# Recurrence output in SBUF, a fourth PSUM bank for short products and a new order table, in a fused cross-attention and RWKV kernel

## The chip, the cores and the metric

The kernel runs on one core of a Trainium2 chip. The metric is the device time of one execution in microseconds (us). The kernel before takes 2110.64 us, the median of three runs (2108.8 to 2110.85).

The engines are called as in the profile: PE does matrix products (PEld are its weight loads), DVE and POOL work element by element, ACT evaluates functions and copies, and SP issues the transfers (DMA). PE writes only to PSUM, a small memory of eight banks; each bank holds 512 fp32 numbers in each of 128 partitions. All other tiles lie in SBUF.

## The reference

Two layers run one after the other on x (32 sequences of 128 rows, 512 wide), all in fp32. The first is cross-attention to `ctx` with a residual and a layer norm. The second, which the change touches, is an RWKV layer; H is 32 heads of S = 16:

```python
xn = _ln(x, ln1_w, ln1_b); sx = _token_shift(xn, state[:, i1])
xxx = tanh((xn + sx * maa_x) @ maa_w1) ... @ maa_w2          # five mixes
x5 = xn[:, :, None] + sx[:, :, None] * (maa_stack + xxx)
w = exp(-exp(time_decay + tanh(x5[1] @ decay_w1) @ decay_w2))
r, k, v = x5[3] @ Wr.T, x5[0] @ Wk.T, x5[2] @ Wv.T;  g = silu(x5[4] @ Wg.T)
def step(s, rkvw):                       # over the 128 rows
    a = k_t[:, :, :, None] * v_t[:, :, None, :]
    out = einsum('bhk,bhkd->bhd', r_t, u * a + s)
    return (a + w_t[:, :, :, None] * s, out)
# group norm over each head, * g, @ Wo.T, residual; then ln2, token shift,
# rr = sigmoid(xr @ Wr2.T); kk = square(relu(xk @ Wk2.T)); x + rr * (kk @ Wv2.T)
```

## The kernel before, in words

The 32 sequences go in 16 groups of two (`G` = 2, so 256 columns, `N`). The first layer runs through all groups; then the second layer does. For each group of the second layer there are three parts, written as functions that only record steps: `front` (norm, token shift, the five mixes `x5`, then the products for k, v, r, the gate and the decay), `recurrence`, and `tail` (group norm, output product, second norm, the three products of the channel mix, store).

**The recurrence** works in four chunks `c` of 128 channels. For each chunk ACT writes the decay into `w4` in PSUM (L1313, two banks, one buffer). Four times per chunk (`dd` = 0 to 3), SP has fetched v, repeated over partitions, into `kv` (L1356, three buffers, each for two `dd`). POOL multiplies it by k (L1379). DVE runs the recurrence over rows as one scan of 1024 columns, out of `w4` and `kv` into `a` (L1395). `a` takes two banks of PSUM and has one buffer. DVE multiplies `a` by r, read out of SBUF and repeated four times, into `ar` in SBUF (L1410, three buffers). After each two `dd`, PE sums `ar` over partitions into `acc` (L1426, one bank). Then DVE adds the current row's own term (L1444), PE centres it (`pc`, L1453), and ACT leaves two results (L1461, L1468).

**PSUM banks**: three for the tag `g`, which every short product of both layers shares (`px5`, `pk`, `pv`, `pr`, `pg`, `pd`, `pc`, `pb`, `ph0`, `pdd`, `pwo`, `pkk`, `prr`, `pkv`, the transposes `pxn`, and so on); two for `a`; one for `acc`; two for `w4`. The tile framework puts in all waits between engines. It also keeps two engines from using one bank of a tile at the same time: the copy of r out of `pr` on ACT (L737) and the product of the same `pr` with k on DVE (L745) are ordered one behind the other.

**The order of the work** is written out when the program is built. Each step has an engine, a work (an estimate of its time in us, from `mm`, `dve`, `act` and `pool_`) and a due time. `Plan.give_out` takes the steps one by one: of the steps whose inputs are made and whose tags have a free place, it takes the one that can start first by its own reckoning, within `ahead` of the oldest due time. Then every engine runs its instructions strictly in this order. The due times come from a table, `WHEN0` for the first layer and `WHEN1` for the second, with one number for each kind of step. The reckoning adds `AFTER` us between engines, and `SWITCH` us where PE changes the shape of its array ("full", "cols", "rows", "turn"). Steps with the tag `g` may take its places in any order (`FREE`).

During the first layer, `beside` puts the loading of the second layer's weights between the steps: transfers on SP (L1170, L1180, L1188) and, for the two weights whose columns change places, a copy on POOL (L1191), through the small pool `wt`.

Of the kernel before, what the change touches and what calls it, by code (L numbers as in the profile page):

```python
# [19 lines left out]
G = 2  # L20
# [57 lines left out]
        att 0: 0.4337, att 1: 0.2346, att 2: 0.4481, att 3: 42.2036, ew 0: 11.1338, ew 1: -0.2147, ew 2: 26.1389,  # L78
        ew 3: -0.1243, gt 0: 26.2110, gt 2: 2.1890, h0: 0.5241, hd: 0.3002, kk 0: 0.9228, kk 2: 20.4292,
        kv 0 0 0: 25.5890, kv 0 0 1: 21.9376, kv 0 1 0: 6.0558, kv 0 1 1: 0.8322, kv 1 0 0: 6.3560, kv 1 0 1: 29.3594,  # L80
        kv 1 1 0: 9.2616, kv 1 1 1: 25.6198, kv 2 0 0: 43.5542, kv 2 0 1: 7.4919, kv 2 1 0: 8.5948, kv 2 1 1: 43.5152,
        kv 3 0 0: 9.4194, kv 3 0 1: 22.4588, kv 3 1 0: 30.1517, kv 3 1 1: 12.4171, pk 0: 26.3643, pk 2: 24.3430,
        pv 0: 22.5942, pv 2: -0.1385, r 0: 26.3795, r 2: 23.3115, rr 0: 40.0790, rr 1: 27.6728, rstd: 26.0489,
        sq 0: -0.1128, sq 1: 23.3775, sq 2: 36.1033, sq 3: 41.1479, w4 0: 25.5550, w4 1: 21.3052, w4 2: 2.5964,
        w4 3: 27.6773, xnc 0: 8.8046, xnc 1: 1.2163, xnc 2: 4.5961, xnc 3: 10.3705, xnt 0: 37.5160, xnt 1: 36.3160,
        xnt 2: -1.1905, xnt 3: 3.6365, xx 0: 20.5242, xx 1: 34.9847, xx 2: 23.3521, xx 3: 22.4330, yk 0: 41.2808,
        yk 1: 20.7056, yk 2: 23.1054, yk 3: 23.1512, yr 0: 42.3101, yr 1: 3.1488, yr 2: 21.3085, yr 3: 2.7447,
        zc 0: 0.7541, zc 1: 27.0647, zt 0: 0.2936, zt 1: 22.7466
    """,
    "DVE": """  # L90
        a 0 0: 23.1285, a 0 1: 44.6967, a 0 2: 19.4777, a 0 3: 17.2122, a 1 0: 22.0121, a 1 1: 24.8715, a 1 2: 8.6631,
        a 1 3: 9.3222, a 2 0: 23.2268, a 2 1: 8.2943, a 2 2: 21.2763, a 2 3: 8.0300, a 3 0: 1.3330, a 3 1: 44.9810,
        a 3 2: 36.5134, a 3 3: 42.7805, ar 0 0: 1.0179, ar 0 1: 22.3833, ar 0 2: 27.7052, ar 0 3: 25.6817,
        ar 1 0: 37.2615, ar 1 1: 13.6436, ar 1 2: 22.7659, ar 1 3: 45.7511, ar 2 0: 6.0171, ar 2 1: 12.5578,
        ar 2 2: 28.8789, ar 2 3: 15.8516, ar 3 0: 23.3130, ar 3 1: 23.1491, ar 3 2: 19.9556, ar 3 3: 32.9812,
        gn 0: 23.7852, gn 1: 20.9580, gn 2: 33.5535, gn 3: 46.4228, gt 0: -0.0231, gt 2: -0.1977, own 0: 5.1099,
        own 1: 0.1224, own 2: -0.0283, own 3: 0.3349, pb 0: 8.0751, pb 1: 2.2968, pb 2: 0.8375, pb 3: 20.4024,
        raw 0: 23.2010, raw 1: 3.5965, raw 2: 23.2455, raw 3: 44.4584, rk 0: -0.7509, rk 1: -0.1719, rr 0: 1.6746,
        rr 1: 1.3382, rstd: 7.6463, st c 0: 11.1186, st c 1: 40.4898, st t 0: 28.5724, st t 1: 15.0321, x1c 0: 2.5303,
        x1c 1: 26.0962, x5 0 0: 2.7039, x5 0 1: 2.7955, x5 0 2: 24.3069, x5 0 3: 21.8074, x5 1 0: -0.0972,  # L100
        x5 1 1: 21.6197, x5 1 2: 0.6004, x5 1 3: 22.4358, x5 2 0: 42.1808, x5 2 1: -0.8591, x5 2 2: 41.2059,
        x5 2 3: 37.6158, x5 3 0: 26.8334, x5 3 1: 24.0914, x5 3 2: 23.6554, x5 3 3: 2.4313, x5 4 0: 25.8630,
        x5 4 1: 22.1314, x5 4 2: 40.0832, x5 4 3: 41.0197
    """,
    "PE": """
        acc 0: 22.3033, acc 1: 7.0581, acc 2: 22.7806, acc 3: 4.9952, pb 0: 27.7390, pb 2: 22.7260, pc 0: 2.0619,
        pc 1: 28.1521, pc 2: 3.1673, pc 3: 23.4917, pd 0: 33.6053, pd 1: 24.8921, pd 2: 20.8375, pd 3: 23.9500,
        pdd: -1.1093, pew 0: 23.8627, pew 2: 5.8633, pg 0: 23.5794, pg 2: 22.0824, ph0: -0.4813, pk 0: -1.0989,
        pk 2: -0.6925, pkk 0: 19.1077, pkk 2: 22.4386, pkv 0: 19.0064, pkv 1: 23.2658, pr 0: 1.2036, pr 2: 2.3445,
        prr 0: 1.8637, prr 1: 21.7968, pv 0: -0.8518, pv 2: 7.2890, pvar: 5.4151, pwo 0: 32.7897, pwo 1: 23.4460,  # L110
        px5 1 0: 39.8845, px5 1 2: 11.2421, px5 2 0: 23.4434, px5 2 2: 23.3758, px5 4 0: 0.9353, pxnc 0: 24.0019,
        pxnc 2: 21.6438, pxnt 0: -1.1522, pxnt 2: 13.7523
    """,
    "POOL": """
        kv 0 0 0: 26.0772, kv 0 0 1: 23.5502, kv 0 1 0: 27.7860, kv 0 1 1: 29.1526, kv 1 0 0: 0.4056,
        kv 1 0 1: 25.8430, kv 1 1 0: 5.7684, kv 1 1 1: 31.4921, kv 2 0 0: 28.2020, kv 2 0 1: 19.5485,
        kv 2 1 0: 29.7046, kv 2 1 1: 42.4003, kv 3 0 0: 10.6540, kv 3 0 1: 4.0853, kv 3 1 0: 25.5882,
        kv 3 1 1: 22.5557, rr 0: 2.4732, rr 1: 44.9550, sd c 0: 18.3198, sd c 1: 13.1243, sd t 0: 33.5214,
        sd t 1: 22.7124, sxc 0: 2.6017, sxc 2: 21.1060, sxt 0: 21.9776, sxt 2: -1.3154, x5 0 0: 41.1636,
        x5 0 2: 2.6161, x5 1 0: 34.2012, x5 1 2: 22.9652, x5 2 0: 22.8432, x5 2 2: 24.0895, x5 3 0: 23.6407,  # L120
        x5 3 2: 27.8090, x5 4 0: 41.2196, x5 4 2: 26.2718, xx 0: 24.1836, xx 2: 9.4476, yk 0: 24.7724, yk 2: 33.3339,
        yr 0: 1.5862, yr 2: 3.3642
    """,
    "SP": """
        fk: 43.5334, fr: 16.5653, kv 0 0 0: 26.7655, kv 0 1 0: 23.9392, kv 1 0 0: 24.5017, kv 1 1 0: 4.2079,
        kv 2 0 0: 5.4685, kv 2 1 0: 28.7358, kv 3 0 0: 28.1974, kv 3 1 0: 22.0650, rr 0: 3.0366, rr 1: 1.8101,
        s0 0: -0.6787, s0 1: 24.2956, vd 0: 11.0274, vd 1: 0.8056, vd 2: -0.1035, vd 3: 13.7197, x1c 0: 41.2264,
        x1c 1: 2.1599, x1t 0: 23.3682, x1t 1: 35.1410
# [13 lines left out]
class Cell:  # L142
# [7 lines left out]
    def __call__(self):  # L150
        return self.t

# [8 lines left out]
class Plan:  # L161
# [15 lines left out]

    def tag(self, name, bufs, space=None):
        kw = {} if space is None else {"space": space}
        pool = self.ctx.enter_context(self.tc.tile_pool(name=name, bufs=bufs, **kw))  # L180
        self.pools[name] = (pool, bufs, [])
# [4 lines left out]
    def add(self, eng, work, fn, r=(), w=(), due=0.0, mode="full", of=None, move=0.0):  # L186
        s = Step(eng, work, fn, due, mode)
# [45 lines left out]

    def _turns(self):

        for s in reversed(self.steps):
            for n in s.behind:
                s.due = min(s.due, n.due - 0.001)
        by_tag = {}
        for s in self.steps:  # L240
            for c in s.fresh:
                by_tag.setdefault(c.tag, {}).setdefault(c, []).append(s.due)
        self.begun = {tag: 0 for tag in by_tag}
        for cells in by_tag.values():
            for i, c in enumerate(sorted(cells, key=lambda c: min(cells[c]))):
                c.turn = i

    def give_out(self, between=()):
        between = list(between)
        for _, _, live in self.pools.values():  # L250
            live[:] = [c for c in live if any(u.end is None for _, _, u in c.uses)]
# [12 lines left out]
        while todo:  # L264
# [3 lines left out]
            for e, ss in ready.items():  # L268
                pick = None
                for s in ss:  # L270
# [3 lines left out]
                    for s0 in s.before:  # L274
                        at = max(at, s0.end + (0.0 if s0.eng == e else self.AFTER[s0.eng]))
# [12 lines left out]
            turn = SWITCH if s.eng == "PE" and s.mode != mode else 0.0  # L288
            if s.eng == "PE":
                mode = s.mode  # L290
            for c in self._places(s)[1]:
                self.pools[c.tag][2].remove(c)
# [54 lines left out]
def xattn_rwkv_kernel(  # L347
# [93 lines left out]
    pl1 = Plan(ctx, tc, WHEN1, 0.7291)  # L441
# [169 lines left out]
    def front(g, D):  # L611
# [120 lines left out]
        for c in range(0, KC, 2):  # L732
# [18 lines left out]
                r=[pp, (g.k, c), (g.k, c + 1)],  # L751
# [51 lines left out]
    with ExitStack() as sa:  # L803
        wa = sa.enter_context(tc.tile_pool(name="wa", bufs=1))
        wt = sa.enter_context(tc.tile_pool(name="wt", bufs=1))
# [369 lines left out]
        for i, (t, w) in enumerate(((wk1, WkT), (wr1, WrT), (fv, fWvT))):  # L1175
# [6 lines left out]
        for d in range(S):  # L1182
            beside(5.0 + 0.12 * d, rows_by_d, d)


        def fetch_wt(tmp, src, c):
            tmp.append(wt.tile([P, E], F32, tag="wtmp", name=f"wtmp_{len(between)}_{c}"))
            nc.sync.dma_start(tmp[0], src[c * P : (c + 1) * P])  # L1188

        def turn_wt(tmp, dst, c):  # L1190
            nc.gpsimd.tensor_copy(  # L1191
                dst[:, c].rearrange("p (c d h) -> p c d h", d=S, h=HC),
                tmp[0].rearrange("p (c h d) -> p c d h", h=HC, d=S),
            )

        for i, (src, dst) in enumerate(((WvT, wv1), (WgT, wg1))):
            for c in range(KC):
                tmp = []
                beside(7.0 + 0.4 * (i * KC + c), fetch_wt, tmp, src, c)
                beside(7.2 + 0.4 * (i * KC + c), turn_wt, tmp, dst, c)  # L1200
# [5 lines left out]
        for i, w in enumerate((wo1, fv)):  # L1206
            for c in range(KC):
                beside(10.4 + 0.2 * (i * KC + c), halve, w, c)
# [61 lines left out]
    pl = pl1  # L1270
    fix = ctx.enter_context(tc.tile_pool(name="fix", bufs=1))
# [4 lines left out]
    pl.tag("a", 1, PSUM)  # L1276
    pl.tag("acc", 1, PSUM)
    add, cell = pl.add, pl.cell
# [19 lines left out]
    w4 = Cell(None, None, "w4", t=t)  # L1298


    def recurrence(g):
# [3 lines left out]
        for c in range(KC):  # L1305
# [16 lines left out]
                due=D - 0.05,  # L1322
            )
# [23 lines left out]
            for dd in range(4):  # L1347
                due = D + 0.06 * dd
                q, e = dd // 2, dd % 2
                if e == 0:  # L1350
# [38 lines left out]
                a = cell("a", [P, 4, G, T], f"a_{n}_{dd}")  # L1389
# [5 lines left out]
                    lambda kv=kv, a=a, e=e: nc.vector.tensor_tensor_scan(  # L1395
# [274 lines left out]
```

## Time and profile before

| what | us |
|---|---|
| median of three runs | 2110.64 |
| the profiled execution, its own time | 2111.21 |
| its span, from the first to the last instruction | 2109.4 |
| first layer | 0 to about 600 |
| transition: end of the first layer, `front` of group 0 | 600 to 677 |
| group 0, from its first scan to that of group 1 | 677 to 751 |
| groups 1 to 14 | 751 to 1977 |
| group 15, to the end of the last scan | 1977 to 2049 |
| `tail` of group 15 | 2049 to 2109.4 |

Read the page from the top: its first part gives the busy time of each engine, its second the same over 40 equal slices. As the four stages have different limits, the view by stage (busy time of each engine in a stretch of time, mean granted clock of PE, share of the DMA engines in use) says more than the totals. The view of waits gives, for one engine and line, the idle time before it and what ended it. The timeline gives one row for each run of equal instructions: start, duration, engine, line, output<-inputs.

From group 1 on, the distance between the first scans of two groups is 86.9 to 88.5 us.

### The profile page before, as it was taken

Reading aid. Unit: us, or ns where it says so; the run is one execution under the profiler, and the core shown is the slowest. Engines: PE = TensorE matmul, PEld = TensorE weight load, DVE = VectorE, ACT = ScalarE, POOL = GpSimd, SP = SyncE. Lnnn points to the kernel's source line nnn. Section 1 sums busy time; section 2 is a strip of 40 time slices with the busy share of each in tenths; the row PEclk is TensorE's granted clock in tenths of the full one; section 3 lists DMA queues with packets and bytes.
Section 4 is the critical chain, followed back from the end, with each engine's and each line's share of the span. In section 5 each row is a group of like instructions: output and inputs, shape, how many; then the busy total and the mean of one; then the engine's idle time right before and its main releaser. Section 6 shows DMA issues by size and latency. Waiting matters only on the chain.

```text
span 2109.4 us, 36165 instructions
## 1 busy us (share of the span) xinstructions
PE 1972.5 (94%) x11908; PEld 1278.1 (61%) x11908; DVE 1784.1 (85%) x2168; ACT 1049.1 (50%) x3473; POOL 1298.3 (62%) x1095
## 2 busy tenths in 40 slices
PE   7999999999988789999999999999999999999976
PEld 5666666667646456656566565665656656566533
DVE  4888888888863998989989889898998989989881
ACT  5888887888852233443433434334343333443232
POOL 1334445343345776868778687776877868778552
PEclk9999999999988799999999999999999999999987
DMA  6232221212116788897988879888798887988870
GB/s 182 91 95 86 83 79 60 61 60 61 44 32 114 117 120 148 137 163 121 162 145 138 160 124 162 144 139 158 125 160 145 137 164 121 158 147 126 155 133 30
DMA packets 156091, 252.23 MB, mean 120 GB/s; under 512 B 50720, under 2 KB 97856, under 8 KB 139520
## 3 DMA queue, kind: packets, MB, share of 16 engines
q1 hardware_dynamic: 155376, 248.88, 64.0%
q8 instruction: 94, 1.54, 0.4%
q14 instruction: 93, 0.76, 0.2%
q10 hardware_dynamic: 528, 1.05, 0.1%
HBM read 224.12 MB, written 25.69 MB: 118 GB/s over the span
## 4 chain that ended last, share of the span: by engine, by line
PE 33%; DMA 15%; DVE 10%; SPq 4%; issue 2%; ACT 1%; POOL 1%; DVEq 0%; POOLq 0%; ACTq 0%
DMA kv<-vd 13%; PE pk L549 5%; PE pkk L549 5%; DVE a L1395 4%; PE pwo L567 3%; PE px L640 3%; PE acc L1426 3%; PE pg L549 3%; PE pv L549 3%; PE pkv L567 2%; SPq L724 2%; DVE ar L1410 2%; SPq L1356 2%; DMA out_dram<-rr 1%; PE pdd L708 1%
## 5 line engine op out<-in xcount | busy, mean ns | idle before, releaser
L1379 POOL TENSOR_TENSOR kv<-kv,kx 128x1016 f32<-128x1016 f32 x256 | 597.4, 2351 | 167.0 <-DMA kv<-vd 127.2
L1395 DVE TENSOR_TENSOR_SCAN a<-w,kv 128x1024 f32<-128x1024 f32 x256 | 586.7, 2292 | 14.6 <-POOL sd_t L415 2.5
L1065 ACT ACTIVATE pr<-pr,mx 128x128 f32<-128x128 f32 x1024 | 396.1, 391 | 40.3 <-DVE mx L1052 40.0
L1410 DVE TENSOR_TENSOR ar<-a,r 128x1024 f32<-128x1024 f32 x256 | 312.5, 1221 | 8.0
L671 POOL TENSOR_TENSOR x<-x,xnt 128x512 f32<-128x512 f32 x160 | 186.5, 1182 | 69.8 <-DVE x L656 69.5
L1065 ACT ACTIVATION_READ_ACCUMULATOR pr<-pr,mx 128x1 f32 x1024 | 194.4, 190 | 0.0
L1039 DVE TENSOR_TENSOR pr<-sc,m 128x1024 f32<-128x1024 f32 x128 | 155.9, 1218 | 17.6 <-PE sc L1023 14.3
L1077 PE MATMUL ppT<-ident,pr 128*128 128x128 f32 x1024 | 151.5, 281 | 14.6 <-DVE v L1000 4.4
L656 DVE SCALAR_TENSOR_TENSOR x<-px,col,sxt 128x256 f32<-128x256 f32 x320 | 134.6, 474 | 35.9 <-PE px L640 33.7
L1426 PE MATMUL acc<-ar,give 128*32 128x256 f32 x2048 | 141.1, 391 | 24.2 <-DVE ar L1410 24.2
L1052 DVE TENSOR_REDUCE mx<-pr 128x8 f32<-128x1024 f32 x128 | 155.0, 1211 | 2.2
L1077 PEld LDWEIGHTS ppT<-ident,pr 128*128 128x128 f32 x1024 | 113.9, 141 | 65.6 <-ACT pr L1065 21.8
L1084 DVE COPY pT<-ppT 128x512 f32<-128x512 f32 x192 | 129.4, 683 | 12.3 <-PE ppT L1077 11.8
L549 PE MATMUL pr<-x,wr 128*128 128x256 f32 x512 | 121.3, 386 | 14.3 <-DVE x L656 13.1
L1130 PE MATMUL pw<-wo,oT 128*128 128x512 f32 x256 | 122.9, 625 | 6.5 <-POOL oT L1125 6.5
L549 PE MATMUL pkk<-yk,fk 128*128 128x256 f32 x512 | 123.1, 389 | 4.9 <-POOL yk L515 4.5
L567 PE MATMUL pwo<-wo,gt 128*128 128x512 f32 x256 | 126.0, 628 | 1.3 <-DVE gt L1508 0.9
L549 PE MATMUL pk<-x,wk 128*128 128x256 f32 x512 | 123.0, 389 | 3.4 <-ACT kx L688 2.9
L965 PE MATMUL pq<-xT,wq 128*128 128x256 f32 x512 | 123.1, 385 | 1.2 <-ACT xT L916 0.7
L549 PE MATMUL pv<-x,wv 128*128 128x256 f32 x512 | 122.8, 389 | 1.2 <-ACT xnt L475 1.2
L549 PE MATMUL pg<-x,wg 128*128 128x256 f32 x512 | 122.8, 388 | 0.5 <-ACT att L1461 0.4
L567 PE MATMUL prr<-fr,yr 128*128 128x512 f32 x256 | 119.2, 599 | 0.7 <-ACT rr L1569 0.7
(146 smaller groups left out, 3527.6 us busy)
## 6 DMA issues: line engine op xcount, KB each, us to landing
kv<-vd SPq DMA_DIRECT2D x1024, 128.0 KB
fk<-in_fWkT_dram SPq DMA_DIRECT2D x16, 1024.0 KB
fr<-in_fWrT_dram SPq DMA_DIRECT2D x16, 1024.0 KB
x<-in_x_dram SPq DMA_DIRECT2D x32, 256.0 KB
ct<-in_ctxT_dram SPq DMA_DIRECT2D x32, 256.0 KB
bc<-rd SPq DMA_DIRECT2D x256, 32.0 KB
x1d<-z SPq DMA_DIRECT2D x32, 256.0 KB
x1t<-x1d SPq DMA_DIRECT2D x32, 256.0 KB
```

The source lines that it names most:

```text
L549: nc.tensor.matmul(pp()[:, i], (w() if isinstance(w, Cell) else w)[:, kc, (c + i) * P : (c + i + 1) * P], flat(src()[:, kc]), start=(kc == 0),
L567: nc.tensor.matmul(pp(), src()[:, c, b, :], (w() if isinstance(w, Cell) else w)[:, c, :], start=(c == 0), stop=(c == KC - 1),)
L656: lambda i=i, c=c, pp=pp, half=half: nc.vector.scalar_tensor_tensor(flat(ts[i]()[:, c]), pp()[:, half], col[:, MS0 + i, c : c + 1], flat(s ...
L671: lambda i=i, c2=c2: nc.gpsimd.tensor_add(ts[i]()[:, c2 : c2 + 2].rearrange("p c b t -> p (c b) t"), ts[i]()[:, c2 : c2 + 2].rearrange("p ...
L1039: lambda b=b, sc=sc, jp=jp, pr=pr: nc.vector.tensor_tensor(pr(), sc()[:, 2 * jp : 2 * jp + 2].rearrange("p j g e s -> p (j g e) s"), ms[b] ...
L1052: lambda pr=pr, mx=mx: nc.vector.tensor_reduce(mx(), pr(), AX.X, ALU.max, negate=True),
L1065: nc.scalar.activation(pr()[:, 4 * i + h, :], pr()[:, 4 * i + h, :], AF.Exp, bias=mx()[:, 4 * i + h : 4 * i + h + 1], accum_out=sm()[:, h0 ...
L1077: nc.tensor.transpose(pt()[:, h, :], pr()[:, 4 * i + h, :], ident)
L1379: lambda c=c, kv=kv, e=e: nc.gpsimd.tensor_tensor(kv()[:, e, :, :, 1:T], kv()[:, e, :, :, 1:T], k()[:, c, :, 0 : T - 1].unsqueeze(1).broad ...
L1395: lambda kv=kv, a=a, e=e: nc.vector.tensor_tensor_scan(a().rearrange("p j b t -> p (j b t)"), w4().rearrange("p j b t -> p (j b t)"), kv() ...
L1410: lambda c=c, a=a, ar=ar: nc.vector.tensor_tensor(ar(), a().rearrange("p j b t -> p j (b t)"), flat(r()[:, c]).unsqueeze(1).broadcast_to([ ...
L1426: nc.tensor.matmul(acc()[32 * j : 32 * j + 32, :N], give[:, d].rearrange("p e h -> p (e h)"), tiles[d]()[:, j], start=(d == 0), stop=(d == 3),
```

## The change

- The scan writes to `ar` in SBUF, and the product with r is done in place in `ar`. The tag `a` is gone. r comes from a new tile `r2` in PSUM (one bank, two halves of 256 columns, for even and odd chunks). A new ACT step for each chunk copies r into it, 64 in all.
- The other bank of `a` becomes a fourth place of the tag `g`, for the second layer only (class `Places`).
- The DVE product `rk` out of `pr` is recorded as behind ACT's copy of r out of the same bank, so the planner counts this wait.
- The planner's works change for the second layer: DVE's times 0.94, POOL's times 0.97, 0.04 us more for each PE step, 0.1 us for a change of shape, and 0.1 us between two DVE steps where one needs the other. The `ahead` is 34.0008 where it was 0.7291.
- All numbers of `WHEN1` are new. `WHEN0` is as it was.
- The pool `wt` is gone: two weights are staged through tiles that are filled later. The transfers and POOL copies are as many as before, at other times in the first layer.

```diff
 WHEN1 = {
     "ACT": """
-        att 0: 0.4337, att 1: 0.2346, att 2: 0.4481, att 3: 42.2036, ew 0: 11.1338, ew 1: -0.2147, ew 2: 26.1389,
+        att 0: 34.1348, att 1: 0.2847, att 2: 27.6851, att 3: 6.8158, ew 0: 12.7301, ew 1: 14.2982, ew 2: 0.1380,
...
+class Places:
+    def __init__(self, free, taken):
+        self.free, self.taken = free, taken
+    def tile(self, shape, dtype, tag, name):
+        self.taken[name] = self.free.pop(0)
+        return self.taken[name].tile(shape, dtype, tag=tag, name=name)
+    def back(self, cell):
+        self.free.append(self.taken.pop(cell.name))
...
+        self.rate, self.begin, self.switch, self.own = {}, 0.0, SWITCH, 0.0
...
+        work = work * self.rate.get(eng, 1.0) + (self.begin if eng == "PE" else 0.0)
...
+    def _after(self, e0, e):
+        if e0 != e:
+            return self.AFTER[e0]
+        return self.own if e == "DVE" else 0.0
...
-                        at = max(at, s0.end + (0.0 if s0.eng == e else self.AFTER[s0.eng]))
+                        at = max(at, s0.end + self._after(s0.eng, e))
...
-    pl1 = Plan(ctx, tc, WHEN1, 0.7291)
+    pl1 = Plan(ctx, tc, WHEN1, 34.0008)
...
-                r=[pp, (g.k, c), (g.k, c + 1)],
+                r=[pp, (g.k, c), (g.k, c + 1), (g.r, c)],
                 w=[g.rk[c // 2]],
...
-        for i, (src, dst) in enumerate(((WvT, wv1), (WgT, wg1))):
...
+        for c in range(KC):
+            beside(6.0 + 0.25 * c, piece, wg1, WvT, c)
+            beside(7.0 + 0.25 * c, turned, wv1, wg1, c)
+            beside(7.1 + 0.25 * c, piece, fv, WgT, c)
+            beside(8.1 + 0.25 * c, turned, wg1, fv, c)
+            beside(9.6 + 0.25 * c, piece, fv, fWvT, c)
...
     pl = pl1
+    pl.rate, pl.begin, pl.switch, pl.own = {"DVE": 0.94, "POOL": 0.97}, 0.04, 0.1, 0.1
...
-    pl.tag("a", 1, PSUM)
     pl.tag("acc", 1, PSUM)
+    pool, bufs, live = pl.pools["g"]
+    more = ctx.enter_context(tc.tile_pool(name="more", bufs=1, space=PSUM))
+    pl.pools["g"] = (Places([pool] * (bufs - len(live)) + [more], {c.name: pool for c in live}), bufs + 1, live)
...
+    r2 = Cell(None, None, "r2", t=wp.tile([P, 2, N], F32, name="r2"))
...
+            add(
+                "ACT",
+                act(N),
+                lambda c=c: nc.scalar.copy(r2()[:, c % 2], flat(r()[:, c])),
+                r=[(r, c)],
+                w=[(r2, c % 2)],
...
-                a = cell("a", [P, 4, G, T], f"a_{n}_{dd}")
                 ar = cell("ar", [P, 4, N], f"ar_{n}_{dd}")
...
-                    lambda kv=kv, a=a, e=e: nc.vector.tensor_tensor_scan(
-                        a().rearrange("p j b t -> p (j b t)"),
+                    lambda kv=kv, ar=ar, e=e: nc.vector.tensor_tensor_scan(
+                        ar().rearrange("p j n -> p (j n)"),
...
-                        ar(),
-                        a().rearrange("p j b t -> p j (b t)"),
-                        flat(r()[:, c]).unsqueeze(1).broadcast_to([P, 4, N]),
-                        ALU.mult,
+                        ar(), ar(), r2()[:, c % 2].unsqueeze(1).broadcast_to([P, 4, N]), ALU.mult
```

## The prediction

> **What bounds the kernel now.** I read the page's first two parts, then the busy times by stage, then the waits of PE in groups 1 to 14, then DVE's timeline.
>
> The page gives PE 94% and DVE 85% over the span, which does not say which of the two sets the pace where.
>
> ```profile
> PE 1972.5 (94%) x11908; PEld 1278.1 (61%) x11908; DVE 1784.1 (85%) x2168; ACT 1049.1 (50%) x3473; POOL 1298.3 (62%) x1095
> ```
>
> The view by stage does. Its columns are start and end, then busy us of PE, PEld, DVE, ACT and POOL with the instructions, PE's granted clock, the share of the DMA engines, GB/s.
>
> ```profile
> 677.00:751.00 74.00, 50.29 (x298) 30.34 (x297) 69.02 (x67) 16.45 (x42) 50.27 (x32) 0.78 0.84 125
> 751.00:1977.00 1226.00, 1184.71 (x6588) 759.00 (x6586) 1108.48 (x1240) 482.16 (x1070) 917.39 (x693) 1.00 0.85 143
> 1977.00:2049.00 72.00, 62.32 (x308) 35.20 (x308) 67.41 (x61) 24.80 (x55) 46.23 (x31) 0.95 0.88 160
> 2049.00:2109.40 60.40, 40.66 (x114) 20.63 (x114) 11.38 (x22) 14.50 (x26) 11.14 (x14) 0.75 0.08 32
> ```
>
> Groups 1 to 14 take 1226 us, 58% of the span. There PE is busy 1184.71, so it idles 41.3 us, at full clock; DVE idles 117.5. PE is the bound there. Groups 0 and 15, at the two ends, are DVE's: 69.0 of 74 and 67.4 of 72.
>
> Next, what PE waits for between 750 and 1977 (total us, times, longest):
>
> ```profile
> PE pr L549 <- DVE x L656: 13.1, 14, 0.9
> PE ph L535 <- DVE x1c L1523: 9.2, 13, 0.7
> PE pb L1492 <- DVE gt L774: 8.2, 12, 0.7
> PE pd L1330 <- DVE gt L774: 6.3, 12, 0.5
> PE pdd L708 <- DVE gt L774: 2.4, 2, 1.8
> ```
>
> These make 39.2 of the 41.4 us of idle time in that view. No operand is late in any of them. `ph0` reads `xx` and a weight, not `x1c`; `pb` reads `rstd` and `pd` reads `rk`, neither reads `gt`; `pr` and `pdd` read `x5`, which POOL (L671) finishes after DVE's L656. What the DVE operations named here have in common is that each empties a place of the tag `g`. So in these groups PE idles for PSUM banks: three are too few.
>
> DVE's timeline shows what waiting on itself costs (start, duration):
>
> ```profile
> 1225.81 2.29 DVE L1395 TENSOR_TENSOR_SCAN a<-w,kv 128x1024 f32<-128x1024 f32 x1
> 1228.13 1.22 DVE L1410 TENSOR_TENSOR ar<-a,r 128x1024 f32<-128x1024 f32 x1
> 1229.46 2.30 DVE L1395 TENSOR_TENSOR_SCAN a<-w,kv 128x1024 f32<-128x1024 f32 x1
> ...
> 1235.68 1.23 DVE L1410 TENSOR_TENSOR ar<-a,r 128x1024 f32<-128x1024 f32 x1
> 1236.82 0.41 DVE L1444 TENSOR_TENSOR own<-acc,own 128x256 f32<-128x256 f32 x1
> ...
> 1242.48 2.29 DVE L1395 TENSOR_TENSOR_SCAN a<-w,kv 128x1024 f32<-128x1024 f32 x1
> 1244.68 1.64 DVE L656 SCALAR_TENSOR_TENSOR x<-px,col,sxt 128x256 f32<-128x256 f32 x4
> ```
>
> From a scan's start to its own multiply is 2.32; to something that does not need it, 2.20. From a multiply to the next scan, which must wait for the one buffer of `a`, is 1.33; to something else 1.14. So being next to the step one needs costs 0.12 and 0.19 us.
>
> **The change, part by part.**
>
> *Fourth place of `g`.* It works on the 41.4 us of PE idle time in groups 1 to 14. From above: all goes, -41. From below: the order is new everywhere, and DVE may be late with operands instead, 0 (worse is a rival). I take 60%, -25: the longest of the frequent waits is 0.9 us, so a free place covers each one, but a PE that runs ahead by a tile soon stands before `acc`, whose `ar` DVE makes. Around the waits some products are stretched: 128x512 ones take a mean of 611, 599 and 593 ns (`pwo`, `prr`, `pkv`, 224 each), 128x256 ones 389, 386, 386, 385 and 382 (448 each). All at their best would be (18+6)x224 + (7+4+4+3)x448 ns = 13 us; I take -4. In the transition PE waits 2.7 us for `kx` (ACT empties a bank, at 639.6) and 1.2 for `xnt` (650.0) before products that read neither: -4.
>
> *The scan into `ar`.* Counting over the order of DVE's instructions: before, 158 multiplies stand right behind their scan and 81 scans right behind a multiply whose `a` they overwrite; after, 62 and 0. DVE time freed: 96 x 0.12 + 81 x 0.19 = 27 us. In groups 1 to 14 it lies beside PE's work and is worth nothing by itself. Groups 0 and 15 are DVE's: 23 such places become 5 and 19 become 3, 34 x 0.15 = -5 us.
>
> Is the scan itself faster or slower into SBUF? No row shows it. Nearest: 128x256 products of a PSUM and an SBUF operand take 418 ns into PSUM (L1500) and 417 into SBUF (L1338): 256 x 0.001, nothing. The multiply still has one operand in PSUM and one in SBUF: 1221 ns (L1410), 1218 (L1039). Bounds +-10 ns for both, 512 x 0.01 = +-5 us of DVE time, +-0.5 at the ends.
>
> *`r2`.* 64 copies of 256 columns by ACT. Nearest rows 380 ns (`sq`, out of PSUM) and 497 (`yr`, SBUF): 24 to 32 us of ACT, busy 482 of 1226. The cover is ACT's idle time. The added wait: ACT's copy for the next chunk stands behind `w4` and waits for the fourth multiply of this chunk; behind it on ACT are copies that empty `g`. `w4` starts when the fourth scan ends and takes 1.02, the multiply ends 1.25 after the scan, so the copy holds ACT some 0.25 us and runs 0.4: 0.65 x 64 = 42 us, hidden; uncovered it would be 0.65 a chunk.
>
> Both halves of `r2` share a bank. In this trace two engines take turns on a bank even when neither needs the other's result: ACT's `r` waits 44.0 us for DVE's `rk`, and `rk` 20.3 for `r`. That `rk` is now recorded behind `r` adds no wait, for it stood there already. But DVE's first multiply of a chunk cannot overlap the copy into `r2`; in the new order a scan (2.2 us) or more stands between them, cost 0. [...]
>
> [...]
>
> *Weights and the rest.* 20 transfers and 8 POOL copies (1.08 us) stay, at other times of the first layer, where POOL is busy 233.7 of 600 and the DMA engines 27%; one copy's wait of 4.3 us goes. The order of PE, ACT and DVE is unchanged there: 0. The tail of group 15 is 57 products behind the last `acc` in both: 0.
>
> **Sum**: -25 - 4 - 4 - 5 = -38 us against the profiled 2111.2 (span 2109.4): 2073.2. The median of the runs is 0.6 lower: 2073.
>
> **Rivals.**
>
> *The place of the wait moves (no change or little).* PE idles as long, now for DVE's products. For it: already now `acc` waits for `ar` in places, and a table's numbers are one search's luck. Against: DVE has 117.5 us of slack in groups 1 to 14 and gains 27. Then only the -5 of the ends stays: 2106.
>
> *`ar` is held too long (slower).* A scan now takes its `ar` buffer a scan earlier than the multiply did, and there are three. In the new order 97 scans wait for PE to have read one out, where 54 multiplies did. PE works in order and `acc` can stand behind eight records of a projection, 1.73 us. If DVE stands on average half of that, 0.87, in each of 64 chunks, it is 56 us, and against -38 that is +18: 2129. It decides from 38/64 = 0.6 us a chunk. Against it: between multiply and blocked scan two further multiplies (2.3 us) often stand.
>
> *The change does not do what it says.* The fourth place is used: 177 tiles lie in that bank. But `r2` may hold up ACT at the wrong place: 32 us of the gain gone, 2105.
>
> **How the numbers follow.** Forecast 0.66 (own range 2046 to 2098), moved wait 0.14, slower 0.14, `r2` 0.06. The low end has all of 41 + 13 + 4 + 5 = 63 us gone, 2048, and 2 us below it for the bounds of the scan and the tail; the range reaches up to 2112 over the moved wait and `r2`, and leaves the slower rival and some of the low side out. A measurement here tells about 0.2%, 4 us, from no change. Faster by more: 0.66 + half of the moved wait + most of `r2` + 0.01 = 0.78; within: 0.08; slower 0.14.
>
> **What would show it.** Right: in groups 1 to 14 PE idles under 20 us and the waits of `ph0`, `pd`, `pb`, `pr` on `x1c`, `gt`, `x` are mostly gone; groups come every 85 to 86 us; scan to own multiply stays at 2.32, fewer of them; `r2` at 0.38 to 0.50 us. Wrong: PE's idle time is there under `ar` (moved wait), or DVE's scans idle for `acc` (slower), or multiplies for ACT (`r2`). I would also be wrong if the scan took over 2.4 us into SBUF, or if the transfers (85% of the DMA engines) did not keep pace with shorter groups.

## The result, and the profile after

The changed kernel takes 2157.88 us, the median of four runs (2156.46 to 2159.18); beside it the kernel before took 2110.74 (2108.8 to 2111.57). The ratio is 1.0231, with a 95% interval of 1.0217 to 1.0245: **slower by 47 us**, where 38 less were forecast. The profiled execution took 2158.39, its span 2156.5.

The page's first part, and the view by stage with the same columns as before (the bounds are the first scans of groups 0, 1 and 15, and the end of the last scan):

```profile
PE 2005.8 (93%) x11908; PEld 1299.9 (60%) x11908; DVE 1759.5 (82%) x2168; ACT 1069.0 (50%) x3537; POOL 1297.3 (60%) x1095
```

```profile
674.90:746.00 71.10, 49.40 (x311) 32.27 (x310) 61.94 (x53) 17.31 (x46) 49.08 (x27) 0.80 0.89 127
746.00:2026.40 1280.40, 1220.77 (x6584) 782.42 (x6577) 1088.48 (x1240) 498.32 (x1123) 913.42 (x691) 0.97 0.82 137
2026.40:2097.80 71.40, 64.31 (x303) 33.87 (x302) 66.95 (x66) 24.83 (x57) 49.13 (x32) 0.93 0.83 140
2097.80:2156.50 58.70, 39.23 (x125) 20.38 (x123) 11.79 (x22) 15.10 (x27) 12.41 (x15) 0.84 0.19 63
```

The ends became shorter, by some 7 us in all where 9 were forecast: the first scan starts at 674.9 (677.1 before), group 0 takes 71.1 (74), group 15 takes 71.4 (72), the tail 58.7 (60.4). All of the loss lies in groups 1 to 14: 1280.4 in place of 1226, **54 us more**. There PE idles 59.6 us (41.3 before), and it is *busy* 36 us longer with the same products, at a mean granted clock of 0.97 (1.00 before). Two things are to be explained, then: a new wait, and a slower PE.

PE's waits in that stretch (total us, times, longest):

```profile
PE px L670 <- DVE own L1379: 31.1, 9, 3.7
PE pkk L579 <- issue: 9.3, 3, 3.1
PE pxnt L497 <- DVE x L686: 5.1, 12, 0.4
PE pkk L579 <- POOL kv L1420: 3.2, 1, 3.2
```

The five waits of before on `x`, `x1c` and `gt` have left the list but for a few us. In their stead stand 13 long ones, 43.6 us, one in each group from 1 to 13, all at the same place of the group. DVE pays behind them:

```profile
DVE own L1482 <- PE acc L1464: 87.0, 25, 7.3
```

One such place, in group 9. Of the names in it, `px5` 2 and 3 are the products for mixes 2 and 3 of the next group, which PE computes in turns; `pd` 1, `own` 1 and `acc` belong to the chunks of the present group; `pkk` is a product of the channel mix. Each product leaves two records in the profile. First PE's timeline (start, duration, in brackets the idle time ahead and what ended it), then DVE's:

```profile
1248.37 1.07 PE L1464 MATMUL acc<-ar,give 128*32 128x256 f32 x16
1249.37 0.69 PE L670 MATMUL px<-h,w 32*128 32x256 f32 x2
1253.62 1.79 PE L670 MATMUL px<-h,w 32*128 32x256 f32 x6 [3.56 <-DVE own L1379]
1255.35 6.35 PE L579 MATMUL pkk<-yk,fk 128*128 128x256 f32 x16
1261.63 1.07 PE L1464 MATMUL acc<-ar,give 128*32 128x256 f32 x16
```

```profile
1246.23 3.45 DVE L1451 TENSOR_TENSOR ar<-ar,r 128x1024 f32<-128x1024 f32 x3
1249.61 2.28 DVE L1435 TENSOR_TENSOR_SCAN ar<-w,kv 128x1024 f32<-128x1024 f32 x1
1251.92 1.22 DVE L1451 TENSOR_TENSOR ar<-ar,r 128x1024 f32<-128x1024 f32 x1
1253.06 0.42 DVE L1379 TENSOR_TENSOR own<-pd,vx 128x256 f32<-128x256 f32 x1
...
1262.77 0.42 DVE L1482 TENSOR_TENSOR own<-acc,own 128x256 f32<-128x256 f32 x1 [7.22 <-PE acc L1464]
```

PE begins `px5` 2 of the next group and stands 3.56 us before `px5` 3, which waits for `own` 1 of the present group. `px5` does not read `own`: what `own` does for it is to empty the bank of `pd` 1, and DVE gets to that only behind a scan and a product. When PE goes on, `pkk`'s 16 records take 6.35 us (3.72 where they run undisturbed). `acc` stands behind `pkk`, and DVE behind `acc`: 7.22 us. The view by stretches around this place shows the clock (third number from the right):

```profile
1243.60:1250.40 6.80, 6.33 (x41) 4.16 (x38) 6.80 (x6) 4.95 (x13) 5.64 (x5) 1.00 0.94 135
1250.40:1253.80 3.40, 0.18 (x2) 0.21 (x4) 3.37 (x4) 1.02 (x1) 3.32 (x2) 1.00 0.59 118
1253.80:1260.70 6.90, 6.90 (x19) 5.08 (x19) 1.49 (x5) 0.58 (x3) 4.43 (x5) 0.51 0.90 115
```

After these 3.4 us, which hold 0.18 us of work, PE was granted half its clock for 6.8 us. Twelve of the 13 places have such a drop, ten of 6.8 us and two of 3.4, together 75 us at half clock, so an estimated 37.5 us of work lost (PE is busy 36 us longer). The kernel before has none from 756 us on to the end of group 14. So the account of groups 1 to 14: 43.6 us of new waits, less the 25.3 by which the others shrank (from 41.3 to 59.6 - 43.6 = 16.0), and 37.5 at half clock, 55.8 in all where 54.4 are measured.

### The profile page after: what moved, and what is told of

It is laid out like the page before. It is cut to its first block, busy times and chain, and to the rows that moved or that the text cites. A ratio compares the mean times of both kernels' runs of the same rounds, so it can differ in the third digit from the quotient of the medians.

```text
span 2156.5 us, 36190 instructions
## 1 busy us (share of the span) xinstructions
PE 2005.8 (93%) x11908; PEld 1299.9 (60%) x11908; DVE 1759.5 (82%) x2168; ACT 1069.0 (50%) x3537; POOL 1297.3 (60%) x1095
## 4 chain that ended last, share of the span: by engine, by line
PE 54%; DMA 19%; DVE 14%; ACT 3%; SPq 3%; issue 3%; POOL 3%; DVEq 0%; POOLq 0%; ACTq 0%
DMA kv<-vd 13%; DVE ar L1435 7%; PE pw L1159 5%; PE pq L994 5%; PE pwo L597 5%; PE pk L579 5%; PE ppT L1106 4%; PE pkk L579 4%; PE pg L579 3%; PE px L670 3%; PE sc L1052 3%; PE acc L1464 2%; DMA vd<-vx 2%; SPq L1397 2%; PE pkv L597 2%
## 5 line engine op out<-in xcount | busy, mean ns | idle before, releaser
L1435 DVE TENSOR_TENSOR_SCAN ar<-w,kv 128x1024 f32<-128x1024 f32 x256 | 579.5, 2279 | 26.4 <-PE acc L1464 6.2
L1451 DVE TENSOR_TENSOR ar<-ar,r 128x1024 f32<-128x1024 f32 x256 | 302.1, 1210 | 2.2
L579 PE MATMUL pkk<-yk,fk 128*128 128x256 f32 x512 | 145.8, 442 | 16.0 <-issue 9.3
L1410 ACT COPY kv<-s 128x8 f32<-128x8 f32 x256 | 42.1, 205 | 204.6 <-DMA vd<-vx 87.3
L579 PEld LDWEIGHTS pkk<-yk,fk 128*128 128x128 f32 x512 | 112.3, 225 | 48.5 <-issue 15.5
```

The source lines that it names most:

```text
L579: nc.tensor.matmul(pp()[:, i], (w() if isinstance(w, Cell) else w)[:, kc, (c + i) * P : (c + i + 1) * P], flat(src()[:, kc]), start=(kc == 0),
L1435: lambda kv=kv, ar=ar, e=e: nc.vector.tensor_tensor_scan(ar().rearrange("p j n -> p (j n)"), w4().rearrange("p j b t -> p (j b t)"), kv()[ ...
L1451: lambda c=c, ar=ar: nc.vector.tensor_tensor(ar(), ar(), r2()[:, c % 2].unsqueeze(1).broadcast_to([P, 4, N]), ALU.mult),
```

## The experiments

**Why does `px5` 3 wait for `own`?** In the order's own reckoning (no measurement, but it decides the order) `px5` 2 and 3 start 39.8 us after the group's first `dd` 0 scan and `own` 1 at 43.3: the reckoning puts `px5` 3 into the bank that `pk` has left, which is free. But the tag `g` is still a pool with three buffers (the fourth place is a pool of its own), and which of the three a tile gets is decided by the framework, not by the reckoning. By the banks in the built program, 90 of 634 steps lie elsewhere than planned, and in 13 groups the bank of `pd` 1 is the one that `px5` 3 (9 times) or `pkk` 0 (4 times) got: the 13 waits above. (For the four ahead of `pkk` the view of waits names no releaser, or POOL; that they are for this bank is read from the built program.) The kernel before has 168 such steps, none at a place that costs over 1 us. So the first theory is the bank, and the rival is the new structure (scan into SBUF, `r2`) with its order.

**pin_after and pin_before: every tile in its planned bank.** Each place of `g` becomes a pool with one buffer. The instructions of all engines, and their order, are the same as without the edit.

```diff
-    pl1.tag("g", 3, PSUM)
+    banks = [ctx.enter_context(tc.tile_pool(name=f"g{i}", bufs=1, space=PSUM)) for i in range(3)]
+    pl1.pools["g"] = (Places(banks, {}), 3, [])
...
-    pl.pools["g"] = (Places([pool] * (bufs - len(live)) + [more], {c.name: pool for c in live}), bufs + 1, live)
+    pool.free.append(more)
+    pl.pools["g"] = (pool, bufs + 1, live)
```

> The kernel after, with one edit: each of the four places of the tag g is a pool of its own with one buffer, so that a tile lies in the bank that the order table's reckoning gave it; order, works and table stay. Theory A (the bank): in the kernel after, px5 2/3 of the next group is planned into the bank of pk, which is free by then, but is built into the bank of pd 1, which DVE empties only behind the fourth multiply of the chunk; the 3.56 us of PE idle time and the 6.8 us of half clock behind it come from this alone. Then the groups come every 86.5 to 87.5 us in place of 91.5, no clock record under 1 is left in groups 2 to 13, the wait of DVE's L1482 for acc falls from 87 us to under 15, and the time is 2084 to 2100. Theory B (the structure): scan into SBUF, r2 and the new order make the groups long whatever bank a tile has; then the time stays at 2145 to 2160 and the 87 us of waits stay.

> The kernel before, with the same edit for its three places. Theory A: there, too, tiles lie in other banks than the table's reckoning gave them (168 steps of 634), but the waits that this makes are under 1 us each, 39 us in all at most; with the edit the groups come every 87.0 us in place of 87.5: 2100 to 2110. Theory B: the bank of a tile does not matter: 2108 to 2113.

pin_after: **2072.63 us** (2070.3 to 2076.02), ratio to the kernel before 0.9824, interval 0.9811 to 0.9837. pin_before: 2096.25, ratio 0.9939 (0.9926 to 0.9951). Groups 1 to 14 of pin_after and of pin_before, then PE's longest waits in pin_after:

```profile
738.60:1941.30 1202.70, 1188.55 (x6581) 761.94 (x6578) 1086.55 (x1240) 498.09 (x1123) 914.46 (x691) 1.00 0.88 146
751.20:1963.80 1212.60, 1186.38 (x6593) 763.41 (x6592) 1109.23 (x1240) 484.87 (x1070) 918.02 (x693) 1.00 0.86 145
```

```profile
PE pwo L598 <- DVE gt L805: 3.3, 4, 1.0
PE pwo L598 <- DVE gt L1548: 2.0, 5, 1.2
```

In pin_after PE idles 14.2 us in 1202.7, and from 742 us to the end of group 14 no clock record is below 1. The place that cost PE 7 us in group 9 (3.56 of waiting, 3.4 by the half clock) now reads:

```profile
1213.12 1.07 PE L1466 MATMUL acc<-ar,give 128*32 128x256 f32 x16
1214.12 1.13 PE L671 MATMUL px<-h,w 32*128 32x256 f32 x8
1215.18 3.72 PE L580 MATMUL pkk<-yk,fk 128*128 128x256 f32 x16
1218.83 1.07 PE L1466 MATMUL acc<-ar,give 128*32 128x256 f32 x16
```

The structure is cleared: with the same instructions in the same order the time falls by 85 us, further than the 58 to 74 that I had expected. The kernel before gains 13 us by the same edit, so part of its bank waits came from the choice of bank too. pin_after is the fastest version of this study.

**own_early: one meeting or many?** The banks stay as the framework chose them; in groups 2 to 12 one DVE instruction moves up by two.

```diff
+            if s.key == "DVE a 1 3" and 2 <= s.group <= 12:
+                own = next(o for o in self.steps if o.key == "DVE own 1" and o.group == s.group)
...
+                    own.fn()
+                    c.t, own.fn = None, lambda: None
             s.fn()
```

> The kernel after with its banks as they were built there (90 steps of 634 in another bank than the order's reckoning has), and one DVE instruction moved in each of the groups 2 to 12: own 1, which empties the bank of pd 1, goes two places up, ahead of the fourth scan and the fourth product of its chunk. All other engines keep their order, every tile its bank. It tells one meeting from many. Theory A1 (the loss is this one meeting of px5 2/3 with the bank of pd 1): PE waits there under 0.5 us, no clock record under 1 in groups 2 to 12, and these 11 groups come at 85.5 to 87 us as with the planned banks: 11 x 5.5 = 60 us less, 2090 to 2105 (the other 3 groups of 14 keep their loss). Theory B1 (the other mis-paired banks cost as much): the groups stay above 89 us, the time above 2120.

2095.31 us (2092.95 to 2101.42), ratio to before 0.9929 (0.9912 to 0.9945): **eleven moved instructions are worth 63 us.** Groups 2 to 12 come every 86.6 us (837.8 to 1790.6 us), at full clock (second view), and PE runs through:

```profile
1228.41 1.84 PE L677 MATMUL px<-h,w 32*128 32x256 f32 x8
1230.18 3.72 PE L586 MATMUL pkk<-yk,fk 128*128 128x256 f32 x16
1233.83 1.07 PE L1471 MATMUL acc<-ar,give 128*32 128x256 f32 x16
```

```profile
837.80:1790.60 952.80, 941.28 (x5196) 600.08 (x5194) 856.27 (x979) 396.64 (x891) 725.82 (x551) 1.00 0.88 147
```

All 90 misplaced steps are still misplaced. So most of the loss, 63 of 85 us, was one meeting per group, in 11 of the 13 groups that had it.

**warm and warm_full: how much of it is the clock?** Both add eight products in front of the place where PE stands, into the half of `px5` 2 that is then overwritten: in the one with 32 rows like `px5`'s own, in the other full ones.

```diff
                     for (i, c), (pp, half, lo) in sorted(at.items(), key=lambda a: a[0][1]):
+                        for _ in range(8 if (i, c) == (2, 0) else 0):
+                            nc.tensor.matmul(
+                                pp()[:, half],
+                                wi[lo : lo + 32, c * P : (c + 1) * P],
+                                hi()[lo : lo + 32, :],
+                                start=True,
+                                stop=True,
+                            )
```

In warm_full the operands are `ident` and `hi()`.

> The kernel after, with work added: the first product of px5 2 (32 rows, 256 columns) is computed 8 times more into the same half of its own bank, in every group, just ahead of the place where PE stands. It tells the two parts of the loss apart. [...] If the clock is not what costs, the added products lie in idle time and change nothing, or add up to 16 x 1.8 = 29 us: 2156 to 2187.

> The kernel after (banks as built there), with work added as in the run with px5 2, but now the eight added products are full ones (128 rows, 128 columns of weights, 256 columns of data, 16 records at 0.216 us each), written into the same half of px5 2 and overwritten. In the run with 32-row products PE never stood still at this place, and its clock was still halved there, mostly for 3.4 us in place of 6.8. Theory A2 (the clock follows how much of the array works, and idle time is only one case): with full products no clock record under 1 is left at this place, pkk's 16 records take 3.6 us again and the wait of L1482 for acc falls from 7.2 to some 4 us per group: 2112 to 2130. Theory B2 (the clock drop is set off by something else at this place, as the step's change of array shape): the drops stay and the time is 2150 to 2165.

warm: 2155.32, ratio to before 1.0231 (1.0215 to 1.0247): 2.6 us less than the kernel after, which lies within the spread of its runs (2154.86 to 2162.46), where I had expected 30 to 42 if filling the idle time alone keeps the clock up. PE's timeline and the clock at this place:

```profile
1248.33 3.71 PE L671 MATMUL px<-h,w 32*128 32x256 f32 x16
1251.89 1.80 PE L678 MATMUL px<-h,w 32*128 32x256 f32 x8
1253.62 5.37 PE L579 MATMUL pkk<-yk,fk 128*128 128x256 f32 x16
```

```profile
1250.10:1253.50 3.40, 3.28 (x18) 2.39 (x16) 3.30 (x7) 1.61 (x4) 2.66 (x3) 1.00 0.79 125
1253.50:1256.90 3.40, 3.40 (x9) 2.66 (x9) 0.74 (x2) 0.00 (x0) 3.24 (x5) 0.51 0.93 118
```

PE never stands still, and its clock is still halved, for 3.4 us in place of 6.8. Here 5.3 us of 32-row products did not keep it up; ten such drops are left in groups 1 to 14, with 3.2 to 3.4 us of PE work in the 3.41 us ahead of each. Full products did keep it up:

```profile
1239.42 3.72 PE L671 MATMUL px<-h,ident 128*128 128x256 f32 x16
1243.07 1.71 PE L678 MATMUL px<-h,w 32*128 32x256 f32 x8
1244.71 3.72 PE L579 MATMUL pkk<-yk,fk 128*128 128x256 f32 x16
```

warm_full: 2132.86, ratio 1.0109 (1.0094 to 1.0124). With 16 x 3.65 = 58 us of needless work it is **25 us faster than the kernel after**; no drop is left at these places:

```profile
747.00:2003.20 1256.20, 1238.47 (x6805) 803.03 (x6802) 1087.55 (x1241) 498.83 (x1123) 914.43 (x691) 1.00 0.84 140
```

The time is 3 us outside of what I expected: in those groups the added 14 x 3.65 = 51 us exceed the 43.6 of idle time that they fill by 7.5, which I had not counted. So the half clock was worth about 25 + 7.5, some 33 us, and the rest of the 78 us between the kernel after and pin_after in groups 1 to 14 is the waiting.

**r_sbuf: what is r in PSUM for?** In pin_after the product reads r out of SBUF; the copies into `r2` stay, unread.

```diff
-                        ar(), ar(), r2()[:, c % 2].unsqueeze(1).broadcast_to([P, 4, N]), ALU.mult
+                        ar(), ar(), flat(r()[:, c]).unsqueeze(1).broadcast_to([P, 4, N]), ALU.mult
```

> The kernel after with every tile in its planned bank, and the product in place reads r out of SBUF in place of r2 in PSUM; ACT's copies into r2 stay, read by nobody, so the order of every engine is the same. It tells what r held in PSUM is worth. No row of any run so far has a DVE product of two operands that both lie in SBUF. Theory A (it does not matter where r lies): 1210 ns plus or minus 10, 2068 to 2077. Theory B (two SBUF operands are slower): each 0.1 us more in the product is 25.6 us of DVE, of which groups 1 to 14 have some 7 us each to spare; above 1.5 us a product DVE becomes the bound and the time passes 2090.

2215.98 us, ratio to before 1.0503 (1.0487 to 1.0518): **143 us slower than pin_after.** The costliest groups of instructions (busy us, mean ns of one) in groups 1 to 14, first of pin_after, then of r_sbuf:

```profile
L1422 POOL TENSOR_TENSOR kv<-kv,kx 128x1016 f32<-128x1016 f32 x225 | 524.9, 2355 | 57.7 <-DMA vd<-vx 23.4 <-DMA kv<-vd 18.9 <-DMA x1c<-x1d 7.3
...
L1453 DVE TENSOR_TENSOR ar<-ar,r 128x1024 f32<-128x1024 f32 x224 | 264.2, 1210 | 1.9
```

```profile
L1422 POOL TENSOR_TENSOR kv<-kv,kx 128x1016 f32<-128x1016 f32 x224 | 597.4, 2688 | 20.6 <-DMA vd<-vx 6.4 <-DMA kv<-vd 6.3 <-DMA x1c<-x1d 5.2
...
L1453 DVE TENSOR_TENSOR ar<-ar,r 128x1024 f32<-128x1024 f32 x224 | 454.7, 2059 | 1.9
```

DVE's product goes from 1210 to 2059 ns and POOL's own from 2355 to 2688. Sorted by what lies beside them, the 46 products that overlap nothing of POOL's take 1205 ns still, and the 111 that lie wholly beside POOL's work 2371. In pin_after, with one operand in PSUM, 121 products wholly beside POOL's work take 1212. POOL's own product takes 2.33 to 2.39 us each time in pin_after; in r_sbuf 146 of 224 still do, and 78 take 3.1 to 3.4. So in r_sbuf the two engines hold each other up: beside POOL's work the product takes 2371 ns with both operands in SBUF, and 1212 with one in PSUM. By what means they do, no run shows. Without r in PSUM the scan's output in SBUF costs these 143 us.

**scan_sbuf and scan_r2: the structure in the old order.** Both are pin_before, its order and three places, with the scan into SBUF and the product in place; scan_sbuf reads r out of SBUF, scan_r2 out of `r2`.

```diff
+                ar.twin = a
...
-                    c.t = pool.tile(c.shape, F32, tag=c.tag, name=c.name)
+                    c.t = c.twin.t if c.twin else pool.tile(c.shape, F32, tag={'a': 'ar'}.get(c.tag, c.tag), name=c.name)
...
+            def hold(c=c, done=[]):
+                if not done and c // 2 in g.left:
+                    done.append(nc.scalar.copy(r2[:, c % 2], flat(g.r()[:, c])))
```

(The `hold` part is in scan_r2 alone; it is called ahead of the chunk's first scan or product that finds r copied.)

> The kernel before with its tiles in their planned banks, and of the change only the scan into SBUF with the product in place, r out of SBUF: order, works, table and three places of g are those of before, no r2. Theory A (the gain over the kernel before comes from the fourth place and the new order, the scan into SBUF alone gives little): groups 1 to 14 stay at 86.1 to 86.6 us, the ends lose the 0.19 us at some 19 places: 2090 to 2097, against 2096 without it. Theory B (the structure is the gain): 2073 to 2085.

> [...] Now r is copied by ACT into r2 in PSUM, once a chunk, ahead of the chunk's first scan (64 copies that the order of before does not count); everything else is the kernel before with its tiles in their planned banks: its order, table and three places of g. Theory A (the rest of the gain is the new order and the fourth place; scan into SBUF and r2 by themselves give the ends a few us): the product is back at 1210 to 1220 ns, groups 1 to 14 stay at 86.1 to 87 us, 2086 to 2098. Theory B (scan and r2 are the gain, the order gives little): 2070 to 2080. Theory C (r2's copies stand in ACT's way at places that the old order did not keep for them): above 2100.

scan_sbuf: 2298.2, ratio 1.0888 (1.0862 to 1.0914). It did not answer its question, as the product took 2004 ns and POOL's own 2596: slower, both of them, as in r_sbuf. scan_r2: 2185.1, ratio 1.036 (1.0339 to 1.0382), with the product back at 1217 ns. That is 89 us *slower* than pin_before, and none of my three theories names the largest wait: `r2`'s copies are not what DVE waits for.

```profile
DVE a L1425 <- PE acc L1456: 109.2, 41, 7.1
```

The scans wait for PE's `acc`: 41 times, 109.2 us (in pin_before DVE waits 2.2 us for `acc` in all, none of it ahead of a scan). A scan into SBUF takes one of the three `ar` buffers a product earlier than the old order allows for. This is the wait that the second rival of the prediction describes, here in another kernel. It is not the whole account:

```profile
748.60:2051.10 1302.50, 1232.37 (x6590) 779.24 (x6589) 1102.52 (x1240) 497.23 (x1129) 918.50 (x693) 0.97 0.81 136
```

PE idles 70.1 us in groups 1 to 14 (26.2 in pin_before), and it is busy 46 us longer: 17 stretches, 65 us in all, are at half clock, though PE never idles longer than 2.7 us there. PE's waits for ACT's `kx` grow from 2.9 to 14.6 us, so a part of theory C stays open, and that the scans' waits bring on the rest was not tried by itself. A fourth `ar` buffer was not tried. The new order avoids the wait: it runs three scans, then their three products, and the fourth scan behind `acc`; in the kernel after scans wait 6.0 us for `acc` in groups 1 to 14.

What the fourth place of `g` is worth apart from the new table was not tried: the old table cannot be laid out with the new structure, nor the new one with three places (steps are left that wait for places).

## Why the prediction was wrong, point by point

- **The step that failed: "From below: the order is new everywhere, and DVE may be late with operands instead, 0 (worse is a rival)", and with it the -25 of groups 1 to 14.** I bounded PE's idle time from below by nothing, and the rival of the moved wait by the same idle time in another place, 2106. Measured are 59.6 us of idle time for 41.3, and 36 us of busy time on top. The wait did move, as that rival said, but its price was wrong twice: one bank that comes 2.5 to 3.7 us late in 13 groups, and a clock that is halved at twelve of these 13 waits. All eight idle times of 3.54 to 3.66 us have a drop of 6.8 us; of the five of 2.47 to 3.19 us four have a drop too, two of 6.8 us and two of 3.4. The twelve drops begin whole multiples of 3.413 us apart. PE need not stand still for them: it was busy for 0.26 to 1.86 us of the 3.41 ahead of each, and in warm for 3.2 to 3.4. I had read the clock by stage, found 1.00, and did not ask what a single longer wait would do to it.
- **"In these groups PE idles for PSUM banks: three are too few": half right.** With planned banks and three places PE idles 26.2 us of 1212.6 (pin_before) in place of 41.3; with four, and the new order, 14.2 (pin_after). A part of the 41.3 was banks badly given, not too few. That the four places are one pool of three and one of one stood in the diff; what follows from it for the choice of bank, I did not look at. The difference could be seen before the run, by comparing the banks in the built program with the reckoning.
- **The mechanism and the size hold once the banks do.** Groups 1 to 14 take 1202.7 in pin_after, 23.3 less than before, against -25 and -4 for stretched products; PE's idle time is under the 20 us named; groups come every 85.9 us, where 85 to 86 was named. That the whole, 2072.63, is what the sum gave is partly luck: it is another kernel, 27 us of idle time went (25 forecast), PE was busy 4 us longer in these groups where 4 less were forecast, and transition, ends and tail gave 18 where 9 were forecast.
- **-4 in the transition:** the first scan is 2.2 us earlier in the kernel after, 4.8 in pin_after. **-5 at the ends:** 2.9 and 0.6 for groups 0 and 15 in the kernel after; in pin_after 7.7 and 3.0, more than the dependent neighbours explain. The new order leaves DVE less to do in group 0, 62.1 us in pin_after (54 instructions) where it was 69.0 (67); in the kernel after it has as little, 61.9, but waits 8.9 us there, and 3.9 with the planned banks. **Tail, 0:** -1.7 and -2.5.
- **The scan and the product:** 2279 ns in place of 2292 and 1210 in place of 1221, just past my 10 ns. **`r2`:** 64 copies of 375 ns, 24.0 us, and 9.3 us of waiting for the fourth product; 33 of the 42 us that I had put down, hidden as assumed. Of two halves in one bank nothing is seen: no product waits for ACT. But I priced `r2` as a cost only and never asked why r should be in PSUM: that is worth 143 us.
- **"`ar` is held too long":** not in this order (6.0 us); in scan_r2 such waits are there, 109.2 us.

## What to carry to other kernels

When a table or a planner counts on a certain buffer, see that the tile really lies there, with one pool for each place if need be; here one tile per group in the wrong bank cost more than the whole change brings. Price a wait on PE by its length, not only by its sum: waits of 0.9 us cost their sum, one of 3.5 us cost that and 3.4 more at half clock here, and in warm a run of 32-row products led to half clock with no wait at all. And before a scan's output goes into SBUF, see what the next DVE operation then reads, and which engine it may then hold up (here 2059 ns a product in place of 1210, and 2688 for POOL's in place of 2355).

## What the runs showed of the hardware

- PE's clock fell without an idle time that the view shows: 5.3 us of 32-row products (16 + 8 records, warm) led to 3.4 us at half clock, where 3.6 us of full products followed by 1.6 of 32-row ones (warm_full) did not.
- In scan_r2 17 stretches of groups 1 to 14 are at half clock, though no idle time of PE there is longer than 2.7 us.
- A DVE product of 128 x 1024 with both operands in SBUF takes 1205 ns alone and 2371 wholly beside POOL's work, and POOL's own product takes 2688 as a mean, where it takes 2355 in pin_after (r_sbuf). With one operand in PSUM the DVE product takes 1207 and 1212 (pin_after).
